# A two-layer graph network: products of zeros at the start, and sixteen buffers for the sums of the query and key weights

## The chip, the cores and the metric

The kernel runs on one core of a Trainium2 chip. A core has TensorE (PE in the profile; its weight loads are listed apart as PEld), VectorE (DVE), ScalarE (ACT), GpSimd (POOL) and SyncE (SP). Each of the last four can also issue DMA transfers, in the order of its own queue; the profile writes such an issue as SPq, ACTq or POOLq, or as a DMA_DIRECT2D instruction. The metric is device time in microseconds (us), the median of several executions.

## The reference

The input x is 128 graphs of 64 tokens with 768 features, all in float32, with a 64 x 64 adjacency matrix for each graph. Two layers follow each other:

- Layer 0: scores u = h h^T / sqrt(768) inside each graph, a softmax, the product with the adjacency, and a normalisation give attn. Three projections h W_left, h W_self and h W_right (768 x 768 each, with bias) are mixed: tokens to the right of a token take the left projection, tokens to its left the right one, and the token itself the self projection. A layer norm with gamma and beta, a relu, a residual and another layer norm end the layer.
- Layer 1: 12 heads of width 64 with projections Wq, Wk and Wv, masked scores plus beta times the adjacency, softmax, the product with v, a residual and a layer norm.

```
ctx = attn_left @ h_left + diag(attn) * h_self + attn_right @ h_right
x   = layernorm(x + relu(layernorm(ctx) * gamma + beta))
x   = layernorm(x + softmax(mask(q k^T / 8 + beta * adj)) @ v)
```

## The kernel before, in words

The 8192 tokens are worked in 16 blocks of 512 tokens (`NBLK`), four tiles of 128 rows each. Projections aren't plain products: `seven` (L522) computes a 2 x 2 block product with seven products instead of eight, `nested` does that twice over, and `products` (L465) computes a 2 x 3 by 3 product with fifteen products (the table `FIFTEEN`). Each such scheme needs sums and differences of blocks of the weights and of the activations. The sums of activations are formed on POOL (`combined`, `fifteen`), those of the weights once, in a prologue, and they are stored in DRAM and read again for every block.

The prologue is what matters here; it covers the first 200 us or so:

- Block 0 is loaded (`loads`, L1200), transposed on TensorE (`transposed`, L397, copied out by ACT in L398), and its scores are computed (`attention0`, L703). The weight matrix W_self is loaded in quarters by SP and `prepare` (L322) forms three differences and one more from them on DVE (L354), each stored by a POOL DMA (L230, L233).
- `self_part(0)` and the two `side_part(0, ...)` are the three projections of block 0, by `seven`: products in L542, evictions on DVE in L575, L767 and L807. The weights W_left and W_right are prepared in the same stretch, into a pool named `prep` of 7 tiles of 4608 bytes a partition and the pool `wst` of 19 tiles of 1536 bytes.
- `prepare1("v", ...)` makes the fifteen sums for Wv in tiles that are free at that time.
- Then the pool `prep` is closed, and a pool `prep1` is opened in its place with 11 tiles of 2048 bytes. `prepare1("q", ...)` and `prepare1("k", ...)` use these tiles for the forms of Wq and Wk, while TensorE computes the three projections of block 1 (L542 again, evicted in L575, L767 and L801).
- After that `streams` is closed, so `wst` and `prep1` end, and the pools of the main part (`wst1`, `l1s`, `l1e`, `l1`, `more`) take that memory. Block 0 is transposed for layer 1 (`transposed1`), its sums are formed on POOL (`fifteen`, L458), and the main loop begins with `values(0)` (L480, evicted in L990).

`prepare1` (L243) works like this. Nine ninths of a weight matrix are loaded by DMAs on the ACT queue (`loaded`, L268), 256 KB each. Fifteen sums follow on DVE (`summed`, L301 and L303), each of which takes a fresh tile; a raw ninth is loaded up to `AHEAD` = 3 sums before it is needed. A ninth or a sum that one of the fifteen products needs is stored by a DMA on POOL's queue (`stored`, L282 and L284). The tile for a new form is the one that has been free for longest:

```
home = min(homes, key=lambda h: h[0])
...
homes.append((done[0] + base + (4 if any(u == x for _, u, _, _ in FIFTEEN) else 0), holder.pop(x)))
```

so a form that is stored counts as free four sums later than one that isn't. When a tile is reused, whoever writes it (a load on the ACT queue or a sum on DVE) waits for all who used it, the store's DMA among them.

In the prologue the order on each engine is laid out by the framework's scheduler at build time, from its own estimates of durations and the order in the program; from `manual_schedule` on (the main loop) it is the order of the program. `step` (L154) takes one piece of side work from a queue after each product; while `recent["bound"]` is set, that work is put behind the last eviction on DVE. `issue_after(x)` puts what a block of code issues on the engine of x behind x in that engine's order.

The memory of a partition at the end of the prologue, counted from the start of `wst`: `wst` 0 to 29184 bytes, `prep1` from 29184 on. In the main part: `wst1` 0 to 24576, `l1s` to 30720, `l1e` to 36864, `l1` (the tile `v` and two `share` tiles) to 52416, `more` (five tiles of 2048 bytes for sums of activations) to 62656.

Of the kernel before, what the change touches and what calls it, by code (L numbers as in the profile page):

```python
# [11 lines left out]
F32 = mybir.dt.float32  # L12
# [5 lines left out]
P = 128  # L18
B, L, D = 128, 64, 768
H, HD = 12, 64  # L20
KC = D // P
HC = KC // 2
HALF = D // 2
# [13 lines left out]
TH = D // THIRDS  # L37
# [33 lines left out]
def gnn_two_layers(ctx: ExitStack, tc, x, adj, wl, bl, ws, bs, wr, br, gamma, beta,  # L71
                   wq, bq, wk, bk, wv, bv, abeta, out):
    nc = tc.nc
# [11 lines left out]
    tmp = ctx.enter_context(tc.tile_pool(name="tmp", bufs=2))  # L85
    st = ctx.enter_context(tc.tile_pool(name="st", bufs=2))
    ps_st = ctx.enter_context(tc.tile_pool(name="ps_st", bufs=2, space=PSUM))
    ps_mm = ctx.enter_context(tc.tile_pool(name="ps_mm", bufs=4, space=PSUM))
# [12 lines left out]
    def column(v, name):  # L101
        t = const.tile([P, KC], F32, tag=name, name=name)
        nc.sync.dma_start(out=t, in_=v.rearrange("(c p) -> p c", p=P))  # L103
        return t

    bias, affine_of = {}, {}

# [30 lines left out]
    def later(key, *fs, queue=lazy):  # L138
        queue.extend((key, f) if callable(f) else (key, *f) for f in fs)

    def act(f):
        return f, "act"
# [9 lines left out]
    recent = {}  # L152
# [24 lines left out]
    def freed():  # L177

        while first:
            first.popleft()[1]()  # L180
# [6 lines left out]
    def settle(key):  # L187

        for queue in (first, urgent, lazy):
            while any(item[0] == key or item[0][0] == key for item in queue):  # L190
                queue.popleft()[1]()
# [7 lines left out]
    streams = ExitStack()  # L199
# [12 lines left out]
    start = ExitStack()  # L212
    prep = start.enter_context(tc.tile_pool(name="prep", bufs=7))
# [22 lines left out]
    def homes_of_v():  # L236

        xT = tp.tile([P, KC, NTOK], F32, tag="xT", name="h_v")
        yield from (xT[:, c, :] for c in range(KC))
        for t in range(T):  # L240
            yield x1_p.tile([P, D], F32, tag="x1", name="h_v")[:, 0 : 2 * TH]
# [150 lines left out]
    def transposed(src, xT, t):  # L392

        for c0 in range(0, KC, 3):
            ps = ps_mm.tile([P, 4, P], F32, tag="mm", name="ps_x")
            for c in range(3):
                nc.tensor.transpose(ps[:, c, :], src[:, c0 + c :: KC], ident)  # L397
            nc.scalar.copy(xT[:, c0 : c0 + 3, t * P : (t + 1) * P], ps[:, 0:3, :])  # L398
# [24 lines left out]
    def combined(xT, n=None):  # L423

        a11, a12 = xT[:, 0:HC, 0:HTOK], xT[:, HC:KC, 0:HTOK]
        a21, a22 = xT[:, 0:HC, HTOK:NTOK], xT[:, HC:KC, HTOK:NTOK]
        s1, s2 = sums[:, 0:HC], sums[:, HC:KC]
        nc.gpsimd.tensor_tensor(s1, a21, a22, ALU.add)  # L428
        nc.gpsimd.tensor_tensor(a21, a11, a21, ALU.subtract)
        S = {1: a11, 2: a12, 4: a22, 5: s1, 6: s2, 7: a21}  # L430
        if n is not None and n >= DEEP:

            S["deep"] = {i: second_level(S[i]) for i in ORDER2[:2]}
        nc.gpsimd.tensor_tensor(s2, s1, a11, ALU.subtract)
        return S

    def combined4(S, n=None):

        S[3] = sums[:, KC : KC + HC]
        last_sum[n] = nc.gpsimd.tensor_tensor(S[3], S[2], S[6], ALU.subtract)  # L440
# [118 lines left out]
    def by_tokens(nm, S, last, in_sbuf=None, hooks={}, begun=None):  # L559

        wt = dict(in_sbuf or {})
        if begun:
            wt[1], begun = begun

        def factors(i, j):
            if i not in wt:
                wt[i] = [weight(f"w{nm}") for _ in range(HC)]
                for k in range(HC):
                    load = nc.sync.dma_start(out=wt[i][k], in_=pieces[nm][i][:, k, :])
                    streamed.setdefault(nm, []).append(load.ins)  # L570
            return [(S[i][:, k, j * P : (j + 1) * P], wt[i][k]) for k in range(HC)]

        def first(j, b, ps, kept):
            u = tmp.tile([P, HALF], F32, tag="u1" if kept else "u0", name="u")
            recent["u"] = evicted[nm] = nc.vector.tensor_tensor(u, ps, bias[nm][:, b * HALF : (b + 1) * HALF], ALU.add)  # L575
            return u

        seven(HALF, factors, first, lambda j, m, n, ps, part: last(2 * m + j, n, ps, part), hooks, begun)
# [106 lines left out]
    def attention0(n, sums=True):  # L685

        blk = blocks[n]
        at = blk["at"]
        if "hT" in blk:
            xT = blk["hT"]  # L690
        else:
            xT = tp.tile([P, KC, NTOK], F32, tag="xT", name=f"hT_{n}")
            for t in range(T):
                transposed(blk["rows"][t], xT, t)

        freed()

        u = ps_mm.tile([P, T, L], F32, tag="mm", name=f"u_{n}")
        for t in range(T):
            for c in range(KC):  # L700
                for g in range(2):
                    tok = slice(t * P + g * L, t * P + (g + 1) * L)
                    nc.tensor.matmul(u[g * L : (g + 1) * L, t, :], lhsT=xT[:, c, tok], rhs=xT[:, c, tok],  # L703
                                     start=(c == 0), stop=(c == KC - 1))
        if sums:
            blk["S"] = combined(xT)
            combined4(blk["S"], n)

        def bc(v):
            return v[:, :, None].to_broadcast([P, T, L])  # L710

        a = l0.tile([P, T, L], F32, tag="a", name=f"a_{n}")
        a2 = l0.tile([P, T, 2, L], F32, tag="a2", name=f"a2_{n}")
        dg = st.tile([P, T], F32, tag="dg", name=f"dg_{n}")
        blk["a2"], blk["dg"] = a2, dg
        z = st.tile([P, T], F32, tag="z0", name="z0")

        def shifted():
            mx = st.tile([P, T], F32, tag="mx0", name="mx0")
            nc.vector.tensor_reduce(mx, u, AX.X, ALU.max)  # L720
            nc.vector.tensor_tensor(a, u, bc(mx), ALU.subtract)

        def exponentials():
            recent["exp"] = nc.scalar.activation(a, a, AF.Exp, scale=1.0 / math.sqrt(D))

        def masked():
            nc.vector.tensor_reduce(z, a, AX.X, ALU.add)
            nc.vector.tensor_tensor(a, a, at, ALU.mult)

        def normed():  # L730

            d = st.tile([P, T], F32, tag="d0", name="d0")
            nc.vector.tensor_reduce(d, a, AX.X, ALU.add)
            nc.vector.scalar_tensor_tensor(d, z, 1e-10, d, ALU.mult, ALU.add)
            rd = st.tile([P, T], F32, tag="rd0", name="rd0")
            nc.vector.reciprocal(rd, d)
            for c in range(2):
                nc.vector.tensor_tensor(a2[:, :, c, :], a, bc(rd), ALU.mult)

        def diagonal():  # L740
            nc.vector.tensor_tensor(a, a2[:, :, 0, :], ident_g[:, None, :].to_broadcast([P, T, L]), ALU.mult)
            nc.vector.tensor_reduce(dg, a, AX.X, ALU.add)

        shifted()
        later(("a", n), act(exponentials), GAP, masked, normed, diagonal, queue=urgent)
# [14 lines left out]
    def self_part(n, in_sbuf, hooks={}):  # L760

        blk = blocks[n]
        o = [x1_p.tile([P, D], F32, tag="x1", name=f"o_{n}_{t}") for t in range(T)]

        def last(t, h, ps, part):
            cols = slice(h * HALF, (h + 1) * HALF)
            recent["u"] = nc.vector.tensor_tensor(o[t][:, cols], ps, bias["s"][:, cols] if part is None else part,  # L767
                                                  ALU.add)

        by_tokens("s", blk["S"], last, in_sbuf, hooks, blk.get("begun"))  # L770
        blk["x"] = o
# [426 lines left out]
    def now(fs):  # L1198
        for f in fs:
            f()  # L1200

    homes = [(-1, home) for home in homes_of_v()]
# [3 lines left out]
    in_sbuf = prepare("s", prep, prep)  # L1206
    bias["s"] = row(bs, "bs")
    edges(0)
    attention0(0)

    while lazy:
# [5 lines left out]
    blocks[1]["rows"] = [rows[:, t, :] for t in range(T)]  # L1217
    in_sbuf_l = prepare("l", wst, prep, (2, 1, 0))
    nc.sync.dma_start(out=bias["l"], in_=bl.partition_broadcast(P))
    self_part(0, in_sbuf)  # L1220
    settle(("w", "l"))
    in_sbuf_r = prepare("r", prep, wst, (4, 0, 3))
    nc.sync.dma_start(out=bias["r"], in_=br.partition_broadcast(P))
# [12 lines left out]
    with tc.issue_after(streamed["b", "r"].ins):  # L1236
        bias["q"], bias["k"] = column(bq, "bq"), column(bk, "bk")
        nc.sync.dma_start(out=abeta_c, in_=abeta.partition_broadcast(P))
    nc.vector.tensor_scalar(abeta_c, abeta_c, SCALE, None, ALU.mult)
    start.close()  # L1240
    prep = streams.enter_context(tc.tile_pool(name="prep1", bufs=11))
    homes = [(-1, prep.tile([P, 2 * TH], F32, tag="h", name="h_qk")) for _ in range(11)]
    now(context0(0)[0])
    attention0(1)


# [304 lines left out]
```

## Time and profile before

| what | before |
|---|---|
| median of 3 executions | 2799.73 us (2798.21 to 2800.53) |
| the profiled execution | 2799.42 us, of which 2797.7 us are the span |
| TensorE busy | 2775.1 us, 99% of the span, 17962 matmuls |
| DVE, ACT, POOL busy | 1934.7, 1115.1, 962.6 us |
| TensorE busy in the first 300 us | 290.09 us |
| mean granted TensorE clock | 0.999 |

The span is the time from the first to the last instruction of the profiled execution. A row of a waits view gives the waiting engine and line, the releaser, the total in us, the number of waits and the longest. A row of a windows view gives the stretch, its length, then busy time and number of instructions (in brackets) for PE, PEld, DVE, ACT and POOL, then the granted clock, the busy share of the DMA engines and GB/s. A row of a timeline gives start, duration, engine, line, operation, output and inputs with shapes, a count, and in brackets the idle time before it with what ended it; rows that follow one another with the same operation are merged.

### The profile page before, as it was taken

Reading aid. Unit: us, or ns where it says so; the run is one execution under the profiler, and the core shown is the slowest. Engines: PE = TensorE matmul, PEld = TensorE weight load, DVE = VectorE, ACT = ScalarE, POOL = GpSimd, SP = SyncE. Lnnn points to the kernel's source line nnn. Section 1 sums busy time; section 2 is a strip of 40 time slices with the busy share of each in tenths; the row PEclk is TensorE's granted clock in tenths of the full one; section 3 lists DMA queues with packets and bytes.
Section 4 is the critical chain, followed back from the end, with each engine's and each line's share of the span. In section 5 each row is a group of like instructions: output and inputs, shape, how many; then the busy total and the mean of one; then the engine's idle time right before and its main releaser. Section 6 shows DMA issues by size and latency. Waiting matters only on the chain.

```text
span 2797.7 us, 49397 instructions
## 1 busy us (share of the span) xinstructions
PE 2775.1 (99%) x17962; PEld 2013.5 (72%) x17962; DVE 1934.7 (69%) x3380; ACT 1115.1 (40%) x1916; POOL 962.6 (34%) x1251
## 2 busy tenths in 40 slices
PE   8999999999999999999999999999999999999998
PEld 5558677686776867768587685867768677686787
DVE  5767668676675766767677676776767668676667
ACT  0014344335343452434525344353433534345244
POOL 3243334415144141432415225061351513415122
PEclk9999999999999999999999999999999999999999
DMA  9687787958769486695866858578585876948543
GB/s 339 199 299 248 216 256 242 264 151 250 208 186 275 142 267 189 196 266 151 268 180 211 249 170 269 159 229 233 182 259 157 249 208 183 279 143 260 177 129 110
DMA packets 394848, 604.88 MB, mean 216 GB/s; under 512 B 49296, under 2 KB 277648, under 8 KB 394608
## 3 DMA queue, kind: packets, MB, share of 16 engines
q1 hardware_dynamic: 338992, 495.73, 59.3%
q0 software_dynamic: 18704, 76.89, 7.6%
q10 hardware_dynamic: 36912, 29.10, 5.1%
q8 instruction: 146, 2.39, 0.4%
q14 instruction: 94, 0.77, 0.1%
HBM read 530.00 MB, written 78.45 MB: 217 GB/s over the span
## 4 chain that ended last, share of the span: by engine, by line
PE 94%; DVE 2%; DMA 2%; issue 1%; SPq 0%; ACT 0%; POOL 0%; POOLq 0%; DVEq 0%; ACTq 0%
PE ps_X L480 26%; PE ps_Y L480 17%; PE ps_Y L836 13%; PE ps_X L836 11%; PE ps_X L542 10%; PE ps_Y L542 8%; PE ps_ctx L879 3%; PE sc L1041 2%; PE u L703 2%; PE ps_y L1104 2%; PE ps_X L588 1%; DMA qk_d<-h_qk 1%; SPq L103 0%; PE ps_x L397 0%; DMA h_qk<-in_L_gnn_Wk_dram 0%
## 5 line engine op out<-in xcount | busy, mean ns | idle before, releaser
L428 POOL TENSOR_TENSOR sums<-hT 128x768 f32<-128x768 f32 x16 | 29.0, 1811 | 790.3 <-PE ps_X L480 775.5
L1074 ACT ACTIVATE eT<-s 32x384 f32<-32x384 f32 x512 | 266.6, 521 | 33.6 <-PE ps_y L1104 17.0
L480 PE MATMUL ps_X<-xT,wqk 128*128 128x256 f32 x1024 | 234.2, 379 | 0.2 <-ACT xT L398 0.2
L890 ACT ACTIVATE unused<-o 128x768 f32<-128x768 f32 x60 | 50.6, 843 | 440.5 <-DMA sq<-in_x_dram 224.4
L610 DVE TENSOR_TENSOR lr<-ps_Y,u_deep 128x384 f32<-128x384 f32 x273 | 151.7, 556 | 95.3 <-PE ps_Y L836 78.8
L1017 ACT ACTIVATE qk<-ps_X,bq 128x256 f32<-128x256 f32 x128 | 60.7, 474 | 386.9 <-PE ps_X L480 386.6
L480 PEld LDWEIGHTS ps_X<-xT,wqk 128*128 128x128 f32 x1024 | 194.5, 190 | 26.8 <-ACT xT L398 0.4
L836 PE MATMUL ps_Y<-wlr,q 128*128 128x384 f32 x546 | 208.5, 491 | 0.0
L1020 DVE TENSOR_TENSOR qk<-qk,ps_X 128x512 f32<-128x512 f32 x160 | 109.5, 685 | 126.7 <-PE ps_X L480 66.9
L1115 POOL TENSOR_TENSOR o<-o,share 128x192 f32<-128x192 f32 x240 | 135.5, 593 | 148.7 <-DVE share L1112 148.7
L480 PE MATMUL ps_Y<-more,wqk 128*128 128x256 f32 x768 | 181.4, 379 | 0.0
L480 PE MATMUL ps_X<-sums,wqk 128*128 128x256 f32 x768 | 180.8, 382 | 0.6 <-issue 0.3
L458 POOL TENSOR_TENSOR more<-xT 128x512 f32<-128x512 f32 x32 | 40.0, 1272 | 374.9 <-DVE xT L416 184.9
L480 PEld LDWEIGHTS ps_Y<-more,wqk 128*128 128x128 f32 x768 | 145.8, 190 | 19.9
L480 PEld LDWEIGHTS ps_X<-sums,wqk 128*128 128x128 f32 x768 | 144.4, 190 | 21.7 <-DVE qk L1020 1.0
L542 PE MATMUL ps_X<-ws,hT 128*128 128x384 f32 x462 | 154.0, 486 | 0.0
L610 DVE TENSOR_TENSOR u_deep<-ps_X,lr 128x384 f32<-128x384 f32 x195 | 107.6, 552 | 66.8 <-PE ps_X L836 57.5
L1020 DVE TENSOR_TENSOR qk<-qk,ps_Y 128x512 f32<-128x512 f32 x160 | 108.3, 677 | 65.5 <-PE ps_Y L480 63.6
L836 PEld LDWEIGHTS ps_Y<-wlr,q 128*128 128x128 f32 x546 | 101.5, 190 | 67.3 <-DVE lr L610 1.1
L836 PE MATMUL ps_X<-wlr,q 128*128 128x384 f32 x364 | 149.1, 491 | 0.0
L1155 ACT ACTIVATE unused<-o 128x768 f32<-128x768 f32 x56 | 47.3, 844 | 224.9 <-POOL o L1115 222.4
L542 PEld LDWEIGHTS ps_X<-ws,hT 128*128 128x128 f32 x462 | 87.7, 190 | 61.0
(278 smaller groups left out, 6341.8 us busy)
## 6 DMA issues: line engine op xcount, KB each, us to landing
wlr<-lr_d SPq DMA_DIRECT2D x819, 192.0 KB, 3.5
wqk<-qk_d SPq DMA_DIRECT2D x480, 256.0 KB, 2.7
wv<-v_d SPq DMA_DIRECT2D x240, 256.0 KB, 5.8
ws<-d_s SPq DMA_DIRECT2D x180, 192.0 KB, 6.9
ws<-in_L_gnn_W_self_dram SPq DMA_DIRECT2D x135, 192.0 KB, 3.9
xa<-in_x_dram SPq DMA_DIRECT2D x64, 384.0 KB, 5.4
out_dram<-o POOLq DMA_DIRECT2D x60, 384.0 KB, 7.8
sq<-in_x_dram ACTq DMA_DIRECT2D x56, 384.0 KB, 8.8
```

The source lines that it names most:

```text
L480: nc.tensor.matmul(ps[:, h, :], lhsT=a, rhs=b, start=start and h == 0 and k == 0, stop=k == len(fs[h]) - 1, skip_group_check=True)
L542: nc.tensor.matmul(ps, lhsT=a, rhs=b, start=(c == 0 and i in (1, 2, 5)), stop=(c == len(fs) - 1), skip_group_check=True)
L610: nc.vector.tensor_tensor(dst, view(ps), add, ALU.add)
L703: nc.tensor.matmul(u[g * L : (g + 1) * L, t, :], lhsT=xT[:, c, tok], rhs=xT[:, c, tok], start=(c == 0), stop=(c == KC - 1))
L836: nc.tensor.matmul(ps, lhsT=a, rhs=b, start=(k == 0 and j in (1, 2, 5)), stop=(k == len(fs) - 1), skip_group_check=True)
L879: nc.tensor.matmul(ps[g * L : (g + 1) * L, 0:HALF], lhsT=blk["aT"][:, t, g * L : (g + 1) * L], rhs=blk["lr"][t][:, g, h * HALF : (h + 1) * ...
L1017: nc.scalar.activation(dst[:, h], ps[:, h, :], AF.Identity, bias=bias["qk"[h]][:, c : c + 1], scale=float(sign))
L1020: nc.vector.tensor_tensor(dst, dst, ps, ALU.add if sign > 0 else ALU.subtract)
L1041: nc.tensor.matmul(sc[t // 2, r][g * L : (g + 1) * L, t % 2, c, :], lhsT=q[rows, c, tok], rhs=k[rows, c, tok], start=True, stop=True)
L1074: nc.scalar.activation(e[to[0], :, to[1]], pairs[rows, :, cols], AF.Exp, scale=1.0 / SCALE)
L1104: nc.tensor.matmul(y[h, r][cols, t, c, :], lhsT=eT[rows, 2 * h + t, c, cols], rhs=by_parity[rows, 2 * h + t, 2 * c + m, g, :], start=True, ...
L1115: nc.gpsimd.tensor_tensor(res, res, share[:, t], ALU.add)
```

## The change

Three edits. First, a tile of zeros is made on DVE at the very start (in the memory of a tile tagged `u0`, which the evictions of L575 use later), and seven float32 products of it with itself, 128 x 128 by 128, go into a PSUM tile that nobody reads. Second, the scores in `attention0` are remembered, and what `self_part(0)` issues on TensorE is put behind the last of them. Third, `prep1` has 16 tiles and not 11.

```diff
+    blank = tmp.tile([P, HALF], F32, tag="u0", name="blank")
+    nc.vector.memset(blank, 0.0)
+    unread = ps_mm.tile([P, 512], F32, tag="mm", name="unread")
+    for _ in range(7):
+        nc.tensor.matmul(unread[:, 0:P], lhsT=blank[:, 0:P], rhs=blank[:, P : 2 * P], start=True, stop=True)
...
-                    nc.tensor.matmul(u[g * L : (g + 1) * L, t, :], lhsT=xT[:, c, tok], rhs=xT[:, c, tok],
-                                     start=(c == 0), stop=(c == KC - 1))
+                    recent["scores"] = nc.tensor.matmul(u[g * L : (g + 1) * L, t, :], lhsT=xT[:, c, tok],
+                                                        rhs=xT[:, c, tok], start=(c == 0), stop=(c == KC - 1))
...
-    self_part(0, in_sbuf)
+    with tc.issue_after(recent["scores"].ins):
+        self_part(0, in_sbuf)
...
-    prep = streams.enter_context(tc.tile_pool(name="prep1", bufs=11))
-    homes = [(-1, prep.tile([P, 2 * TH], F32, tag="h", name="h_qk")) for _ in range(11)]
+    prep = streams.enter_context(tc.tile_pool(name="prep1", bufs=16))
+    homes = [(-1, prep.tile([P, 2 * TH], F32, tag="h", name="h_qk")) for _ in range(16)]
```

## The prediction

> **What bounds the kernel now.** I read the page first, for the engine that has no time to spare, then the waits of TensorE, then busy time by stretch of the prologue, and last the timeline where TensorE stands.
>
> ```profile
> span 2797.7 us, 49397 instructions
> PE 2775.1 (99%) x17962; PEld 2013.5 (72%) x17962; DVE 1934.7 (69%) x3380; ACT 1115.1 (40%) x1916; POOL 962.6 (34%) x1251
> ```
>
> TensorE is idle for 2797.7 - 2775.1 = 22.6 us in all, and no edit takes a product of the real work away. So what the change can win lies in these 22.6 us, or in products that run slower than they could.
>
> The waits of TensorE over the first 300 us, with their releasers:
>
> ```profile
> PE ps_x L397 <- DMA xa<-in_x_dram: 4.8, 2, 4.1
> PE ps_X L542 <- DVE u L575: 1.5, 2, 1.0
> PE ps_Y L542 <- DVE lr L807: 1.4, 1, 1.4
> PE ps_Y L542 <- DVE lr L801: 0.8, 1, 0.8
> ```
>
> Busy time by stretch (the first number after the length is PE):
>
> ```profile
> 14.00:24.00 10.00, 9.93 (x31) 5.62 (x30) 9.61 (x12) 0.42 (x1) 8.63 (x6) 1.00 1.05 372
> 24.00:54.00 30.00, 30.00 (x94) 17.61 (x93) 16.45 (x34) 0.00 (x0) 3.76 (x7) 1.00 1.01 344
> 54.00:64.00 10.00, 7.61 (x23) 4.01 (x22) 9.34 (x19) 0.00 (x0) 5.96 (x11) 1.00 0.96 305
> 112.00:176.00 64.00, 64.00 (x207) 37.91 (x204) 51.23 (x106) 1.91 (x3) 22.06 (x27) 1.00 0.87 274
> 176.00:192.00 16.00, 14.68 (x46) 8.01 (x45) 9.50 (x23) 3.99 (x5) 6.91 (x10) 1.00 0.86 294
> ```
>
> The reader should see two places where TensorE stands: 54 to 64 us, and 176 to 192 us, where the forms of Wk are being made. From 14 to 64 us the DMA engines are busy for all of the time (0.96 to 1.05), so that stretch goes by its transfers. The chip's first products, in the timeline of PE:
>
> ```profile
> 4.06 2.82 PE L397 MATMUL ps_x<-ident,xa 128*128 128x128 f32 x12 [4.06 <-DMA xa<-in_x_dram]
> 7.61 2.82 PE L397 MATMUL ps_x<-ident,xa 128*128 128x128 f32 x12 [0.73 <-DMA xa<-in_x_dram]
> 10.36 3.38 PE L703 MATMUL u<-hT 128*64 128x64 f32 x96
> ```
>
> and the second stand, in the timeline of all engines:
>
> ```profile
> 180.41 0.20 ACT L518 ACTIVATE std<-std 128x4 f32<-128x4 f32 x1 [54.89 <-DMA qk_d<-h_qk]
> 180.65 0.18 DVE L519 RECIPROCAL rstd<-std 128x4 f32<-128x4 f32 x1 [4.51 <-ACT std L518]
> ...
> 181.32 2.20 PE L542 MATMUL ps_Y<-wr,sums 128*128 128x384 f32 x6 [0.79 <-DVE lr L801]
> ...
> 184.06 8.06 PE L542 MATMUL ps_X<-wr,hT 128*128 128x384 f32 x24 [0.54 <-DVE u L575]
> ```
>
> This last one is a whole chain. ACT's square root (L518) stands in ACT's queue behind loads of Wk's ninths (L268), and these wait for a tile whose store (qk_d<-h_qk) has to land. DVE's next instruction needs the root and stands for 4.51 us, the evictions L801 and L575 queue up behind it, and TensorE waits 0.79 and 0.54 us for its PSUM banks.
>
> **The zeros.** One memset on DVE (128 x 384) and seven products. The 48 score products of the program are 96 instructions in the profile, so seven float32 products are 14. A 384-column instruction of L542 follows the one before after 0.32 us (12 in 3.87 us), so one of 128 columns takes about 0.11 us at that pace and 0.22 us at half of it: 14 of them take 1.5 to 3.0 us. TensorE's first data land at 4.06 us and DVE's own first work is at 1.52 us, so all of it lies in time in which both wait; without that cover it would cost up to 3.0 us. Even if the zeros run to 4.4 us and push the first transposes by 0.4 us, the second twelve wait for their DMA until 7.61 us (0.73 us of slack), so nothing is lost.
>
> What they can win: the first 24 transposes follow one another at 2.82/12 = 0.235 us, those of block 1 (24 in 3.61 us, from 105.61 us) at 0.15 us, where ACT's copies set the pace. The view of the granted clock says 1.00 in all these stretches, so I read the slow start from the durations alone: 421 ns against 299 ns for one transpose. The second twelve would end 12 x 0.085 = 1.0 us sooner and the scores, 3.38 us here and 3.02 us in block 1, another 0.4 us: the first product of L542 could start at 12.2 us and not at 13.67. But then TensorE runs into DVE. DVE is busy for 9.61 of the 10 us from 14 to 24, its differences of W_self begin when quarters land at 13.30 and 14.86 us, and the eviction that frees the bank for the second half of the third product ends at 23.64 us, behind them. TensorE waits for it already. So 1.4 us earlier at 13.67 us is 0 us earlier at 23.7 us, and what would be left is lost at 54 us, where DVE waits 6.1 us for W_right's DMA. I take 0 us; the ends are 0 and -1.4 us (if the scheduler, seeing other times, lays DVE's work out so that the lead lives on).
>
> The Trainium skill, "TensorE: Matmul & The Clock Gate", Part 1 (The HAM clock gate), speaks against the zeros: the array is at half clock until one free-running activity window of about 3.4 us has been busy, and a window of idleness takes it back, so 3.0 us of zeros alone fill no window. Part 4 (PE-mode transpose) of that page says that transposes do not count as such activity; by it the zeros win 0 us and the sum stays, while without it the transposes carry on what the zeros began and the sum could be 1.4 us lower. This trace speaks against Part 4: scores start in groups of 8 to 12 a quarter microsecond until 11.2 us and of 16 from there on, 0.8 us after the first of them, too soon for scores alone.
>
> **The order of self_part(0).** In the profile the scores (10.36 us) already stand ahead of L542 (13.67 us) on PE. The edge adds no semaphore, being on one engine. 0 us; it only pins an order that the zeros could have upset, and queues past nothing.
>
> **Sixteen buffers.** No instruction is added or taken away: 18 loads, 30 sums (36 instructions) and the same stores, on the same queues (ACT, DVE, POOL). Following the rule for homes by hand: with 11 tiles Wq needs a used tile from its 12th form on, and Wk's nine loads all wait for tiles of Wq or of early Wk; with 16 only one load of Wq does, and Wk's loads take tiles that were freed three to six sums earlier. So the square root at 180.41 us should come soon after its input (DVE L515, 172.19 us), DVE's 4.51 us of standing go, and with them TensorE's 0.79 + 0.54 = 1.33 us. This is the surest term: -1.3 us.
>
> Around it more is lost than the waits show. From 174.57 to 195.99 us TensorE does 60 instructions of L542 at 0.3225 us = 19.35 us in 21.42 us: 2.1 us lost. Beyond the 1.33 us, some 0.7 us are evictions that came late behind sums waiting for stores (DVE waits 5.1 us there). I take half: -0.4 us; ends 0 and -0.7.
>
> Next in line is the passage to the main loop. DVE's first eviction of v (L990) waits 5.9 us for a store, until 203.14 us, ACT's first copy (L786) until 203.45 us, and PE's sixteen ps_ctx products take 4.1 us (206.06 to 210.16) where the next sixteen take 2.80: 1.3 us lost. By the rule for homes the last form of Wk leaves the memory of v (tile 3 of 11) for that of l1e (tile 1 of 16), so v is free some 3 us sooner. But the copies of ACT are put down to another transfer (w_deep), which needn't move. I take -0.3 us, nearer to nothing, since what ends the wait on ACT isn't one of these tiles; ends 0 and -1.3.
>
> The added tiles have a price as well. `more` lies at 52416 to 62656 bytes, eleven tiles of `prep1` end at 51712, sixteen at 61952. So the sums of activations at 198.31 us on POOL must now wait for the stores of tiles 11 to 15, which they didn't before. By the rule the latest form in them is 21; its store is issued at 193.69 us and lands, at the 5.5 us of the last store, at about 199.2 us. The first sum uses tiles 11 and 12 (forms 16 and 17, stored before 190 us): 0 us. Upper end: it waits as v does, to 203.1 us, 4.8 us late, of which POOL's lead over TensorE at 202.5 us absorbs 0.4: +4.4 us.
>
> **Sum.** 0 + 0 - 1.3 - 0.4 - 0.3 + 0 = -2.0 us. The profiled execution took 2799.42 us, 0.3 us under the median; from the median it is 2799.73 - 2.0 = 2797.7 us. A measurement of this kernel can tell about 0.2% (5.6 us) from no change, so this counts as the same.
>
> **Rivals.** (A) Nothing moves: ACT's root stays behind the loads because their order, not their tiles, is what holds it (a load of Wk is issued only three sums ahead, and the sums are paced by evictions). For it: POOL's stores also wait for loads to land (8.1 us at 171.31). Against: the root's releaser is a store. 2799.5 us.
>
> (B) Slower: `more` waits for late stores, as priced: the sums on POOL start up to 4.8 us late and TensorE, which takes its first sum at 202.51 us, stands up to 4.4 us. For it: the addresses overlap, and v shows this very wait. Against: the late forms lie in other tiles. It decides once the store that matters lands after 200.8 us (the 2.0 us won, and 0.4 of lead, are then gone). With it 2799.73 - 2.0 + 4.4 = 2802.1 us.
>
> (C) Faster: the early lead survives (-1.4), and all of the losses from 174 to 210 us go (-1.3 - 0.7 - 1.3): 2799.73 - 4.7 = 2795.0 us. Against: 14 to 54 us goes by DVE and DMA.
>
> (D) The scheduler uses the freer tiles to pull sums into 138 to 160 us, where DVE is busy nine tenths. 112 to 176 us has no idle time of PE now; six sums (0.68 us each) pulled there cost at most 4.1 us: 2801.8 us.
>
> **How the numbers follow.** Chances: the forecast (2796 to 2799) 0.50, A (to 2800.5) 0.17, B 0.10, C 0.13, D 0.10. Leaving a tenth out at each side, the range goes from 2794.8 (C with its ends) to 2802.3 (B). Below 2794.1 us would take more than all the terms together: 0.04. Above 2805.3 us would take B and D together or a prologue laid out anew, and half of the chance of that is 0.09. The rest, 0.87, is the same.
>
> **What would show it.** Right: in the changed profile the root L518 near 172 us with no store as releaser, no wait of DVE on it, no wait of PE at L801 and L575 near 181 us; transposes from 7.6 us on at about 300 ns; yet the product near 23.7 us in its old place. L990 freed near 200 us. Wrong: POOL's first L458 waiting for qk_d, waits of PE on DVE between 112 and 176 us, or the stand at 54 to 64 us gone, which I hold to be set by the DMA engines.

## The result and the profile after

The changed kernel takes 2804.45 us (median of 21 runs, 2801.58 to 2806.29), the kernel before beside it 2799.5 us (21 runs). The ratio is 1.0019 with a 95% interval from 1.0013 to 1.0025: 5 us slower, a little under what I had called measurable, yet clear of no change with so many runs. I had forecast 2797.7 us and a range up to 2802.3. The profiled execution took 2804.47 us, 5.05 us more than the one of before, and its span is 5.1 us longer, so the trace can be asked for all of the difference.

From the page after, the span and the engines:

```profile
span 2802.8 us, 49419 instructions
PE 2778.2 (99%) x17976; PEld 2017.4 (72%) x17976; DVE 1933.0 (69%) x3381; ACT 1114.5 (40%) x1916; POOL 961.2 (34%) x1251
```

TensorE has the 14 added instructions of the zeros (17976 against 17962). It is idle for 24.6 us and not 22.6, and busy for 3.1 us longer. These totals don't tell where the time went: the zeros alone are 3.35 us of busy time in which TensorE stood before. The stretches have to be looked at one by one.

The waits of TensorE in the first 300 us:

```profile
PE ps_X L486 <- POOL sums L464: 5.5, 1, 5.5
PE ps_X L548 <- DVE u L581: 1.6, 2, 1.0
PE ps_Y L548 <- DVE lr L813: 1.5, 1, 1.5
PE unread L110 <- DVE blank L107: 1.4, 1, 1.4
```

The first row is new and has one entry of 5.5 us: the first products of `values(0)` that read a sum of activations (L480 before, now L486) stand for POOL (`fifteen`, L458 before, now L464). The evictions L801 that held TensorE at 181 us are gone from the list. The busy time by stretch (after the length: PE, PEld, DVE, ACT, POOL, then the granted clock, the DMA share, GB/s):

```profile
14.00:24.00 10.00, 9.06 (x28) 4.78 (x26) 9.61 (x12) 0.42 (x1) 8.63 (x6) 1.00 1.07 371
112.00:176.00 64.00, 64.00 (x220) 38.00 (x217) 52.31 (x109) 2.11 (x4) 21.97 (x27) 1.00 0.92 302
176.00:192.00 16.00, 16.00 (x51) 9.43 (x50) 9.98 (x23) 3.78 (x4) 7.95 (x11) 1.00 0.60 201
192.00:212.00 20.00, 14.45 (x61) 11.64 (x60) 4.95 (x9) 13.03 (x20) 11.35 (x12) 0.83 0.65 218
```

From 176 to 192 us TensorE is now busy throughout (14.68 of 16.00 before), so the gain that I forecast is there. From 192 to 212 us it is busy for 14.45 of 20.00 us, where the same stretch of before has this row, with half as many products again:

```profile
192.00:212.00 20.00, 19.77 (x94) 14.23 (x93) 8.22 (x16) 11.59 (x18) 15.79 (x16) 1.00 0.68 239
```

The granted clock has fallen to 0.83 there. In steps of 2 us, after:

```profile
202.00:204.00 2.00, 0.00 (x0) 0.00 (x0) 1.42 (x3) 1.94 (x3) 1.92 (x2) 1.00 1.05 398
204.00:206.00 2.00, 0.00 (x0) 0.00 (x0) 0.00 (x0) 1.94 (x3) 1.98 (x4) 0.76 1.05 373
206.00:208.00 2.00, 1.31 (x3) 1.13 (x4) 0.00 (x0) 1.90 (x4) 2.00 (x3) 0.50 0.68 219
208.00:210.00 2.00, 2.00 (x6) 1.53 (x6) 0.00 (x0) 1.94 (x3) 2.00 (x2) 0.50 0.00 0
210.00:212.00 2.00, 2.00 (x7) 1.57 (x6) 0.69 (x1) 1.94 (x3) 2.00 (x3) 0.53 0.23 30
212.00:214.00 2.00, 2.00 (x13) 1.08 (x13) 0.86 (x2) 0.26 (x1) 2.00 (x3) 1.00 0.29 109
```

And the timeline of all engines around the stand (start, duration, what, and in brackets the idle time before it with what ended it):

```profile
190.16 0.73 POOL L290 DMA_DIRECT2D qk_d<-h_qk  x1 [2.55 <-DVE h_qk L309]
...
196.03 0.72 POOL L290 DMA_DIRECT2D qk_d<-h_qk  x1 [3.15 <-DVE h_qk L307]
...
201.53 0.69 DVE L996 TENSOR_TENSOR v<-bv,ps_X 128x512 f32<-128x512 f32 x1 [5.80 <-DMA qk_d<-h_qk]
...
202.08 2.48 POOL L464 TENSOR_TENSOR more<-xT 128x512 f32<-128x512 f32 x2 [5.32 <-DMA w_deep<-d_l]
...
204.58 0.77 POOL L385 DMA_DIRECT2D lr_d<-d_l  x1
...
205.37 2.48 POOL L464 TENSOR_TENSOR sums<-xT,more 128x512 f32<-128x512 f32 x2
...
206.69 6.26 PE L486 MATMUL ps_X<-wv,sums 128*128 128x256 f32 x16 [5.55 <-POOL sums L464]
...
212.89 2.80 PE L885 MATMUL ps_ctx<-lr,a 128*64 128x384 f32 x16
...
222.72 2.80 PE L885 MATMUL ps_ctx<-lr,a 128*64 128x384 f32 x16
```

The same steps before, with DVE's first `v` and ACT's first copy:

```profile
198.31 2.51 POOL L458 TENSOR_TENSOR more<-xT 128x512 f32<-128x512 f32 x2
...
200.89 2.48 POOL L458 TENSOR_TENSOR sums<-xT,more 128x512 f32<-128x512 f32 x2
...
202.51 3.62 PE L480 MATMUL ps_X<-wv,sums 128*128 128x256 f32 x16
203.14 0.69 DVE L990 TENSOR_TENSOR v<-bv,ps_X 128x512 f32<-128x512 f32 x1 [5.88 <-DMA qk_d<-h_qk]
...
203.45 0.83 ACT L786 COPY swap<-lr 64x768 f32<-64x768 f32 x1 [3.72 <-DMA w_deep<-d_l]
...
217.20 2.80 PE L879 MATMUL ps_ctx<-lr,a 128*64 128x384 f32 x16
```

What the reader is to see: POOL issues the last store of Wk's forms at 196.03 us and is free at 196.75 us; before, its first sum followed directly behind that issue. Now it starts 5.3 us later, half a microsecond after DVE's `v`, which names that store as its releaser. In between TensorE runs dry, its clock is halved, and its next 16 products take 6.26 us where they took 3.62.

The path in numbers, after against before. POOL's first sum starts 3.77 us later (202.08 against 198.31). The memset of `v` and an issue for `lr_d` now stand between POOL's second and third sum (in the trace of before they come after all the sums), so the third sum starts 4.48 us later (205.37 against 200.89). TensorE's products started 1.62 us behind that sum before and start 1.32 us behind it now, so 0.30 us of it was slack, and they are 4.18 us later (206.69 against 202.51). The half clock adds 2.64 (6.26 - 3.62). The first ps_ctx products no longer catch up with ACT's copies and take 2.80 and not 4.1 us (206.06 to 210.16 before): -1.3. That is 4.18 + 2.64 - 1.3 = 5.5 us, and the second group of ps_ctx products starts 5.52 us later (222.72 against 217.20). The span is 5.1 us longer.

### The profile page after: what moved, and what is told of

Same layout as the page of the kernel before. It is cut to its first block, busy times and chain, and to the rows that moved or that the text cites. A ratio compares the mean times of both kernels' runs of the same rounds, so it can differ in the third digit from the quotient of the medians.

```text
span 2802.8 us, 49419 instructions
## 1 busy us (share of the span) xinstructions
PE 2778.2 (99%) x17976; PEld 2017.4 (72%) x17976; DVE 1933.0 (69%) x3381; ACT 1114.5 (40%) x1916; POOL 961.2 (34%) x1251
## 4 chain that ended last, share of the span: by engine, by line
PE 95%; DVE 2%; issue 1%; DMA 1%; SPq 1%; ACT 0%; POOL 0%; POOLq 0%
PE ps_X L486 26%; PE ps_Y L486 17%; PE ps_Y L842 13%; PE ps_X L842 11%; PE ps_X L548 11%; PE ps_Y L548 9%; PE ps_ctx L885 3%; PE sc L1047 2%; PE ps_y L1110 2%; PE u L709 2%; PE ps_X L594 1%; DMA adj<-in_adj_dram 0%; PE ps_a L760 0%; DVE qk L1026 0%; DVE lr L813 0%
## 5 line engine op out<-in xcount | busy, mean ns | idle before, releaser
L486 PE MATMUL ps_X<-xT,wqk 128*128 128x256 f32 x1024 | 234.2, 379 | 0.2 <-ACT xT L404 0.2
L486 PEld LDWEIGHTS ps_X<-xT,wqk 128*128 128x128 f32 x1024 | 194.5, 190 | 26.7 <-ACT xT L404 0.4
L486 PE MATMUL ps_Y<-more,wqk 128*128 128x256 f32 x768 | 181.4, 379 | 0.0
L486 PE MATMUL ps_X<-sums,wqk 128*128 128x256 f32 x768 | 180.8, 382 | 0.6 <-issue 0.3
L464 POOL TENSOR_TENSOR more<-xT 128x512 f32<-128x512 f32 x32 | 40.0, 1268 | 381.1 <-DVE xT L422 229.2
L486 PEld LDWEIGHTS ps_Y<-more,wqk 128*128 128x128 f32 x768 | 145.8, 190 | 19.9
L486 PEld LDWEIGHTS ps_X<-sums,wqk 128*128 128x128 f32 x768 | 144.3, 190 | 21.6 <-DVE qk L1026 1.0
```

The source lines that it names most:

```text
L486: nc.tensor.matmul(ps[:, h, :], lhsT=a, rhs=b, start=start and h == 0 and k == 0, stop=k == len(fs[h]) - 1, skip_group_check=True)
```

## Experiments

Two theories. **The overlap**: the five added tiles lie in the memory that `more` takes, so POOL's first sum must wait for `prep1`. In the compiled program of the kernel before that sum waits for ACT alone, which writes its inputs; in the changed one it waits for 14 semaphores (counters by which the program makes one engine wait for another, or for a transfer), among them all eight that POOL's stores count up. None of the 14 is waited for up to a load of w_deep, the transfer that the profile names. **The rivals**: that the zeros or the order edge delay something at the start that is paid later; that the number of tiles makes the scheduler lay the prologue out worse; and, once the half clock was seen, that the clock and not POOL is the price.

### The parts alone: sixteen buffers, zeros with their order, twelve buffers

Three kernels, made from the one before.

```diff
 (e_buffers)
-    prep = streams.enter_context(tc.tile_pool(name="prep1", bufs=11))
-    homes = [(-1, prep.tile([P, 2 * TH], F32, tag="h", name="h_qk")) for _ in range(11)]
+    prep = streams.enter_context(tc.tile_pool(name="prep1", bufs=16))
+    homes = [(-1, prep.tile([P, 2 * TH], F32, tag="h", name="h_qk")) for _ in range(16)]
```

> Only the sixteen tiles, no zeros. Theory (the five added tiles lie where `more` lies, and the first sum of activations on POOL waits for everything that used the closed pool): the whole loss is here; POOL's first sum after the pool's end starts near 202 us, PE waits about 5.5 us for it, the products after it run at half clock, and the time is 4 to 6 us above before. Rival (the zeros shift the prologue's start and the loss comes from there): within 1 us of before or faster by 2.

Measured: 2804.51 us (11 runs), ratio 1.002 (1.0011 to 1.0029). The buffers alone cost all of the 5 us. The same wait of TensorE and the same slow products are there:

```profile
PE ps_X L480 <- POOL sums L458: 5.4, 1, 5.4
```

```profile
206.06 6.45 PE L480 MATMUL ps_X<-wv,sums 128*128 128x256 f32 x16 [5.43 <-POOL sums L458]
```

The second has the first and the second edit of the change, and 11 tiles:

```diff
 (e_zeros)
+    blank = tmp.tile([P, HALF], F32, tag="u0", name="blank")
+    nc.vector.memset(blank, 0.0)
...
+    for _ in range(7):
+        nc.tensor.matmul(unread[:, 0:P], lhsT=blank[:, 0:P], rhs=blank[:, P : 2 * P], start=True, stop=True)
...
+    with tc.issue_after(recent["scores"].ins):
+        self_part(0, in_sbuf)
```

> Only the zeros and the order of self_part(0), eleven tiles. Theory: the first L542 starts some 0.8 us sooner, DVE takes it back by 24 us, and the time is within 1 us of before. Rival (the zeros cost what the changed kernel lost): 2804 us. A third reading (the 0.4 us by which the changed kernel was late from 14 to 175 us is the zeros' doing): 2800 us, with that lateness in its profile again.

Measured: 2799.41 us (11 runs), ratio 1.0003 (0.9994 to 1.0012): no difference that these runs can tell. In its timeline the zeros run first, and yet the second half of the third product (L542 before) waits for the same eviction on DVE at nearly the same time, 23.31 us where it was 23.7:

```profile
1.39 3.36 PE L110 MATMUL unread<-blank 128*128 128x128 f32 x14 [1.39 <-DVE blank L107]
...
23.31 2.20 PE L548 MATMUL ps_X<-t_s,sums 128*128 128x384 f32 x6 [0.65 <-DVE u L581]
```

The first product of L542 starts 1.5 us sooner (12.20 us), not 0.8. Of the third reading nothing is seen: the product that the changed kernel had at 174.96 us, 0.39 us late, is at 174.30 us here, with the same zeros.

The third kernel has 12 tiles:

```diff
 (e_twelve)
-    prep = streams.enter_context(tc.tile_pool(name="prep1", bufs=11))
-    homes = [(-1, prep.tile([P, 2 * TH], F32, tag="h", name="h_qk")) for _ in range(11)]
+    prep = streams.enter_context(tc.tile_pool(name="prep1", bufs=12))
+    homes = [(-1, prep.tile([P, 2 * TH], F32, tag="h", name="h_qk")) for _ in range(12)]
```

> The kernel before with twelve tiles and not eleven: the pool ends at 53760 bytes, 1344 bytes into `more`. Theory (overlap by the pool, whatever the number): POOL's first sum waits for the last store of Wk just as with sixteen, PE stands 4 to 6 us near 202 us, and the time is 5 to 8 us above before, as one tile wins little at 181 us. Rival (the loss grows with the number of tiles, by what their earlier loads and sums do to DMA and DVE): a fifth of the changed kernel's loss, 1 us.

Measured: 2808.33 us (6 runs), ratio 1.0031 (1.0019 to 1.0042). One added tile costs as much as five, and more: 9.2 us, where 5 to 8 were expected. The profiled execution took 2805.56 us, so its trace holds only a part of that. In its waits of TensorE the new row is there as before, and in its timeline the stand before the products:

```profile
PE ps_X L480 <- POOL sums L458: 5.8, 1, 5.8
```

```profile
192.71 0.72 POOL L284 DMA_DIRECT2D qk_d<-h_qk  x1 [1.28 <-DVE h_qk L301]
...
196.58 0.72 POOL L284 DMA_DIRECT2D qk_d<-h_qk  x1 [3.15 <-DVE h_qk L301]
...
202.90 2.48 POOL L458 TENSOR_TENSOR more<-xT 128x512 f32<-128x512 f32 x2 [5.59 <-DMA w_deep<-d_l]
...
207.52 6.56 PE L480 MATMUL ps_X<-wv,sums 128*128 128x256 f32 x16 [5.82 <-POOL sums L458]
```

What follows. It isn't how many tiles there are, but that `prep1` reaches into the memory of `more` at all: twelve tiles end at 53760 bytes, 1344 past the start of `more`. This run also speaks to what exactly is waited for. In the compiled program the one tile that lies there (51712 to 53760 bytes) holds form 21 of Wk last; following the rule for homes by hand gives form 15, wrongly, because ninths of Wk are loaded while sums for Wq are still being made. Of DVE's three two-part sums for Wk (forms 15, 21 and 23, at 181.80, 191.66 and 195.53 us in this trace) it is the second; its store is issued at 192.71 us, and form 22, the last sum that reads the tile, is made at 193.59 us. No store issued from 180 us on took longer than 5.8 us to land, so form 21's had landed by 198.5 us. If a tile were released by its own last use, POOL would not have waited beyond that. It started at 202.90 us, 5.6 us after it was through with issuing the very last store (196.58 us), and that store is of another tile (49664 to 51712 bytes), outside `more`. So what is waited for is the closed pool as a whole. The 12 semaphores that the first sum waits for in this version's compiled program say the same: the last store's is among them. Why the rest of the kernel is slower still than with sixteen tiles I didn't follow up; TensorE stands 1.99 us for an eviction (L575) at 177 us, which is the old chain around Wk's loads, here not mended.

### The added tiles in a pool of their own

From the changed kernel: the five added tiles form a second pool behind the first, and Wk's late forms do not go there, so that nothing late is stored from it.

```diff
 (e_own)
+            usable = [h for h in homes if nm != "k" or done[0] < 6 and i not in (7, 9) or not any(h[1] is e for e in early_homes)]
-            home = min(homes, key=lambda h: h[0])
+            home = min(usable, key=lambda h: h[0])
...
-    prep = streams.enter_context(tc.tile_pool(name="prep1", bufs=16))
-    homes = [(-1, prep.tile([P, 2 * TH], F32, tag="h", name="h_qk")) for _ in range(16)]
+    prep = streams.enter_context(tc.tile_pool(name="prep1", bufs=11))
+    early = streams.enter_context(tc.tile_pool(name="prep2", bufs=5))
+    homes = [(-1, prep.tile([P, 2 * TH], F32, tag="h", name="h_qk")) for _ in range(11)]
+    homes += [(-1, early.tile([P, 2 * TH], F32, tag="h", name="h_early")) for _ in range(5)]
+    early_homes[:] = [h for _, h in homes[11:]]
```

> The changed kernel, its five added tiles in a pool of their own that Wk's forms leave after the sixth sum (forms 7 and 9, which are read late, never take one). The memory and the overlap with `more` are the same, but what `more` must wait for is over by 195 us. Theory: PE's wait of 5.5 us and the half clock go, the gain at 181 us stays: 2797 to 2798 us, 2 us under before. Rival (POOL is late because DMA or the order of its queue changed, not because of the pool's end): still 2803 to 2805 us.

Measured: 2797.38 us (11 runs), ratio to before 0.9997 (0.9988 to 1.0006); on the same chip the sixteen tiles in one pool took 2804.51. The wait for POOL is gone, POOL starts its first sum at 196.04 us (202.08 in the changed kernel), and the products run at full clock:

```profile
196.04 2.52 POOL L466 TENSOR_TENSOR more<-xT 128x512 f32<-128x512 f32 x2
...
200.43 3.69 PE L488 MATMUL ps_X<-wv,sums 128*128 128x256 f32 x16
204.05 1.52 PE L887 MATMUL ps_ctx<-lr,a 128*64 128x384 f32 x8
205.79 2.37 PE L887 MATMUL ps_ctx<-lr,a 128*64 128x384 f32 x8 [0.22 <-ACT lr L795]
```

The transfer w_deep, which the changed kernel's row names as POOL's releaser, is issued only at 196.03 us here, and POOL doesn't wait for it. So the late stores in the pool whose memory `more` takes carry the whole loss: the same sixteen tiles in the same memory, with the late forms in a pool that `more` doesn't reach, are 7.1 us faster. (The second pool and the rule that keeps late forms out of it came together; the one without the other was not run.) Against the kernel before, the median is 1.75 us lower, about what I had forecast for the change, but the interval holds no change too. The ps_ctx products still take 4.1 us (204.05 to 208.16), as before.

The same without the zeros and the order edge:

```diff
 (e_own_nozeros, from e_own)
-    blank = tmp.tile([P, HALF], F32, tag="u0", name="blank")
...
-    with tc.issue_after(recent["scores"].ins):
-        self_part(0, in_sbuf)
+    self_part(0, in_sbuf)
```

> Sixteen tiles, five of them in a pool of their own, without the zeros and without the order of self_part(0). Theory (the zeros win nothing that lasts): 2797 to 2798 us, within 0.7 us of the same kernel with zeros. Rival (the zeros have a part in the gain): 1 us or more above it.

Measured: 2797.86 us (11 runs), ratio 0.9996 (0.9987 to 1.0005). That is within 0.5 us of the one with zeros; the zeros win nothing that these runs can tell.

### Is it the clock or POOL?

From the changed kernel: 26 products of the identity into a PSUM tile that nobody reads, put where TensorE stands, so that its clock stays up. POOL is left as late as it is.

```diff
 (e_warm)
+        if n == 0:
+            def busy():
+                idle = ps_mm.tile([P, 512], F32, tag="mm", name="idle")
+                for _ in range(26):
+                    nc.tensor.matmul(idle[:, 0:P], lhsT=ident, rhs=ident, start=True, stop=True)
+
+            at(val, 2, busy)
```

> The changed kernel with 26 products of the identity matrix with itself on TensorE (52 instructions, some 5.6 us, into a PSUM tile that nobody reads), put where TensorE waits for POOL's first sums. Theory (the 5.5 us of idle time let the clock fall to half, and the sixteen products after it took 6.3 us and not 3.6 for that reason): the granted clock stays at 1.00 through 200 to 212 us, the sixteen products take 3.6 us, and the time falls by 2.6 us to about 2802 us. Rival (those products were slow for another reason, their weights or POOL): 2804.5 us.

Measured: 2803.95 us (11 runs), ratio to before 1.0019 (1.001 to 1.0028). I had expected some 2802. The timeline of TensorE:

```profile
200.36 5.97 PE L1415 MATMUL idle<-ident 128*128 128x128 f32 x52
206.58 3.72 PE L486 MATMUL ps_X<-wv,sums 128*128 128x256 f32 x16 [0.25 <-POOL sums L464]
210.23 2.80 PE L885 MATMUL ps_ctx<-lr,a 128*64 128x384 f32 x16
213.98 1.99 PE L486 MATMUL ps_Y<-wv,sums 128*128 128x256 f32 x8 [0.94 <-POOL sums L464]
```

The fill keeps the clock up, as meant (the granted clock is 1.00 in every row from 200 to 214 us): the 16 products take 3.72 us and not 6.26. But then TensorE waits 0.94 us for POOL's next sum, and ps_Y starts at 213.98 us where it started at 215.62: 1.6 us won in this stretch and not 2.5, and in the median 0.5 us, which is less than these runs resolve (the ratio to before is 1.0019, as for the changed kernel). So by the trace a third of the 5 us is the clock at most, and the median shows less. The rest is POOL: its later sums carry its late start on, and the products, slow or fast, have to wait for them. Where the 1.1 us between this stretch and the median went I can't say from these runs.

### Can the passage be made faster than before?

In `e_own` the ps_ctx products still stand for ACT's copies (L786 before), which wait for the last of `prep1`. So I laid six tiles that are free early at the front, under `l1s`, and ten behind them, opened `more` directly after `l1s`, and kept ACT's first copy behind its copies to xT and the memset of `v` behind POOL's sums.

```diff
 (e_front, from e_own)
+    early = streams.enter_context(tc.tile_pool(name="prep2", bufs=6))
+    prep = streams.enter_context(tc.tile_pool(name="prep1", bufs=10))
...
     l1s_p = ctx.enter_context(tc.tile_pool(name="l1s", bufs=1))
+    more_p = ctx.enter_context(tc.tile_pool(name="more", bufs=1))
...
+        with tc.issue_after(recent["xT"].ins):
+            nc.scalar.copy(swap[0:L, 0:D], high)
...
+    with tc.issue_after(recent["sum"].ins):
+        recent["ones"] = nc.gpsimd.memset(v[:, :, :, HD], 1.0)
```

> A version that tries to take all of it: six early tiles in a pool of their own that lies first, ten late ones behind it, `more` moved ahead of `l1e`, so that `l1s` (ACT's swap tile) and `more` meet only the early pool; the swap is kept behind the copies of xT and the fill of v with ones behind POOL's sums. Theory (ACT's first swap waited for the pool's end too): the swap starts near 198 us and not at 201.5, the first sixteen ps_ctx take 2.8 us and not 4: about 2796 us, 1.2 us under the version with two pools. Rival (ACT waits for the transfer it is put down to, w_deep, or ten late tiles are too few): no gain over that version.

Measured: 2798.01 us (11 runs), ratio 0.9996 (0.9987 to 1.0005), where 2796 was expected. ACT's first copy starts at 199.25 us and no longer waits, while DVE's `v`, whose memory `prep1` still meets, waits for the last store until 203.03 us; so ACT's copies too had waited for `prep1`, and not for w_deep, which their row names before. The ps_ctx products now take 2.80 us, and TensorE runs into POOL's next sum:

```profile
199.25 0.83 ACT L795 COPY swap<-lr 64x768 f32<-64x768 f32 x1
...
205.72 2.80 PE L888 MATMUL ps_ctx<-lr,a 128*64 128x384 f32 x16
209.13 1.99 PE L488 MATMUL ps_Y<-wv,sums 128*128 128x256 f32 x8 [0.61 <-POOL sums L466]
```

Of the 1.3 us won, 0.61 are given to that wait; the 0.7 us that remain are less than these runs resolve, and the median shows nothing of them. The same without the zeros (`e_front_nozeros`, with the lines of the last short diff taken out of `e_front`):

> The same without the zeros and without the order of self_part(0). Theory: within 0.7 us of the one with zeros, about 2796 us. Rival (the zeros win): 1 us or more above it.

Measured: 2797.95 us (11 runs), ratio 0.9998 (0.999 to 1.0007). The four versions in which `more` has nothing late to wait for lie at 2797.4 to 2798.0, each 1.3 to 1.8 us below the kernel before in the median and none clear of it by its own interval. None of the versions run is shown to be faster than the kernel before. Another place for `more` outside the memory of `prep1` was not tried.

## Why the prediction was wrong, point by point

- **The zeros, 0 us: held.** `e_zeros` shows it, and by the stated reason: the lead at the start ends at the eviction on DVE at 23 us (the second half of the third product starts at 23.31 us with the zeros, and at 23.20 us in `e_buffers`, without them). Their 14 instructions took 3.35 us, over the 1.5 to 3.0 of the sum, and the slack before the second twelve transposes covered that. Whether they warm TensorE depends on the execution: the first 12 transposes take 1.92 us in `e_zeros` but 2.72 us in the changed kernel, with the same zeros (2.82 before), and `e_buffers`, without zeros, ran its second 12 in 2.03 us. The warm-up varies by as much as the zeros could win.
- **The order edge, 0 us: held.** TensorE's order around it is the same with and without.
- **The chain at 181 us, -1.3, and the evictions around it, -0.4: held in mechanism; the size is known to about 1 us.** The root (L524 now) runs at 172.48 us, DVE no longer waits for it, and the stretch from 176 to 192 us has no idle time. At 175 us the changed kernel is 0.39 us behind, at 190.44 us it is 1.52 us ahead (the same product was at 191.96 before): 1.9 us won where I said 1.7. But `e_zeros`, with eleven tiles too, takes 16.49 us over the same products (174.30 to 190.79 us), before takes 17.39 and the changed kernel 15.48, so by these profiles the chain costs an eleven-tile kernel 1.0 to 1.9 us. The term of 0.4 also leaned on a wrong reading: of DVE's 5.1 us of waits for stores, 4.48 lie before that stretch, at 165 us, and 0.58 in it.
- **The passage, -0.3: 0.** I expected `v` to be free some 3 us sooner. It starts 1.61 us sooner (201.53 against 203.14), by what TensorE's and DVE's earlier work had won, and still waits for the very last store. In `e_own` the ps_ctx products take 4.1 us as before, and where `e_front` freed them half of it went into POOL's next sum, which I hadn't named as next in line.
- **"The added tiles have a price as well ... 0 us": this step failed.** I had the overlap, its addresses and the place where it would tell, and then priced it tile by tile, by a list of forms made by hand: the first sum uses tiles 11 and 12, whose stores were issued before 190 us. Both parts were wrong. The list was wrong: in the compiled program the latest form in the added tiles is 23 and not 21, in the last of them (59904 to 61952 bytes), and its store is the very last. And the release isn't by tile: the 2048 bytes that the first sum writes (52416 to 54464) meet two tiles whose latest store, form 20's, is issued at 190.16 us, and still the sum starts at 202.08 us. The program waits for the closed pool as a whole, so for the last store of all. A row of the profile of before could have said so: DVE's `v` waited 5.88 us for a store, and by the compiled program that store, form 23's, is of a tile outside the memory of `v` (29184 to 31232 bytes; `v` begins at 36864). My list had put it in tile 3, inside `v`, so the wait looked like one for its own tile. And I took the label w_deep at ACT's copies (3.72 us) as evidence that they wait for something else; `e_front` shows that they don't.
- **Rival B's price.** The mechanism was B's, with a chance of 0.10, and the price was short too: 2802.1 against 2804.45. Net of the lead, I had POOL's products +2.4 us late; they are 4.18 late. POOL is released 0.55 us after `v` (why, no run shows), the memset and the issue put 0.71 us between its sums, and the lead counts for less than I took off: `v` comes 1.61 us sooner and not 2.0. Then comes the half clock, 2.64 us less the 1.3 that the ps_ctx products win back, which wasn't in that price at all. The time fell outside the range, 2.15 us over its upper end.
- **Rivals A, C and D didn't come.** The root's wait went (A), the early lead didn't survive (C), and 112 to 176 us stayed full (D).

## To carry to other kernels

When a pool grows, list whose memory it now reaches into, and take as the release time of that memory the last use of anything in the old pool, its slowest store included, unless a run shows finer release. Read which tile lies where from the compiled program; a list made by hand was wrong here. Tiles that are free early are worth a pool of their own, kept free of late forms (7.1 us here between one pool and two). And when an engine that feeds TensorE starts late, price the stand, then TensorE's restart at a lower clock, and then the feeding engine's next piece: what a remedy for the clock alone (`e_warm`) or for ACT's copies alone (`e_front`) won was in part taken by POOL's next sum.

## What the runs showed of the hardware

- The granted clock fell to half while TensorE stood: idle from about 201.1 us, the rows have 1.00 up to 204 us, 0.76 from 204 to 206 (half of it at about 205, if it falls in one step, 4 us after the last product), 0.50 from there, and 1.00 again from 212 us, some 5.2 us after work came back at 206.69. The Trainium skill, "TensorE: Matmul & The Clock Gate", Part 1 (The HAM clock gate), says the same of the kind of thing, a throttle that idleness brings back and work releases, and puts the release at around 4 us into the work; here it took about a microsecond longer.
- The view of the granted clock says 1.00 in the first microseconds as well, where before's transposes took 235 ns each and the second twelve of `e_buffers`, with nothing but twelve transposes on TensorE before them, took 169 (12 in 2.03 us). There the durations tell, not the clock column.
- The last store landed 5.4 us after its issue, where the four stores issued from 186 us on, it among them, have a median of 2.6. SP issued eleven loads between 194.5 and 200.5 us. That these loads are the cause was not tested by a run of its own.
